# A two-layer attention and convolution kernel: the first attention of layer 1 as a pipeline of two tiles, a new order at the seam of the layers, and the 3x3's weights prepared on VectorE alone

## The chip, the cores and the metric

The kernel runs on one core of a Trainium2 chip. A core has five engines that run their own instruction queues side by side and wait for one another through semaphores: TensorE (PE in the profile; its weight loads are PEld), VectorE (DVE), ScalarE (ACT), GpSimd (POOL) and SyncE (SP), which here only issues DMA transfers. The metric is the time of one execution on the device in microseconds; lower is better. Everything is fp32, apart from some operands of layer 0 that are rounded to fp32r.

## What is computed

The input is x of shape (2, 256, 64, 64): two images ("batches") of 256 channels and 4096 positions. Two layers follow each other, each with a group norm in front and a residual sum behind. Layer 0 is ordinary attention with 8 heads over all 4096 positions. Layer 1 is a mix of two branches (cut to what matters here):

```python
# layer 0: 8 heads, softmax over 4096 keys, residual
q, k, v = split(qkv_w @ groupnorm(x) + qkv_b)
x = x + softmax(q^T k * d**-0.5) v
# layer 1, on y = groupnorm(x)
q, k, v = conv1x1(y), conv1x1(y), conv1x1(y)
# first attention: 64 sets of 64 positions, one from each 8x8 block
ctx   = sa(blockify(q * hd**-0.5 + pos), blockify(k + pos), blockify(v))
feats = relu(conv1x1(ctx) * scale + shift)
# second attention: within each 8x8 block; q and k from two layers of conv1x1+bn+relu
ctx2  = sa(qx(feats), kx(feats), conv1x1(feats))
att   = relu(conv1x1(ctx2) * scale + shift)
# convolution branch: q, k, v mixed by fc, then a grouped 3x3
conv  = grouped_conv3x3(mix(q, k, v, fc_w), dep_w)
out   = x + rate1 * att + rate2 * conv
```

The kernel folds q, k, v, the mixing and the grouped 3x3 into one dense 3x3 convolution whose weights it works out itself from fc, dep and the three 1x1 weights.

## The kernel before, in words

The image is held as 8 tiles of 512 positions (T) with the channels as 2 chunks of 128 partitions (KC). The batches run one after the other, and each goes through the same stages:

1. **Start and projections of layer 0** (`group_stats`, `project0`): statistics on VectorE (L326, L330), means over a group and variances by small matmuls with a constant matrix (pm_l L333, pv_l L343), a square root on ScalarE (L346), normalised tokens xn (L368), then keys, values and queries (p_wk L418 is the first). In batch 0, `fold_scores` (L227 to L242) stands ahead of the statistics; it multiplies small weight matrices together for the first attention of layer 1, which is 1,150 us later.
2. **Attention of layer 0**: 16 groups of a head and half of the queries, 32 blocks of keys each. Scores (L511), exp on ScalarE (L517), values av (L527). The sums of rows for softmax are added up by VectorE (L564) and by accumulating DMAs, then summed over partitions by matmuls with ones (`sum_rows`).
3. **The seam** (`finish_last` from L620, `layer1_first` from L1088): the last group's sums of rows (tile `rows`), their reciprocal (L638), a copy that is kept (L639), the scaled values plus the residual (L641, L642), statistics of these (L644), and the aggregate (L330). Then means and variances again, and x is normalised into `xg` in the order that the first attention wants (L1100 on ScalarE, L368 on VectorE). The first channel chunk can be normalised before the second, whose statistics end last. In batch 0, `fold_products` (pt_w, pm_w, pt_fv, pm_fv, pb_lr, L263 to L283) is mixed in: it multiplies the layer's weight matrices.
4. **First attention of layer 1** ("lr"): 8 tiles. For a tile: py (L1134, L1138, the folded query and key projection of `project`), sp (L1029, L1035, scores), pvs (L1011, values), a softmax on VectorE and ScalarE (nm L1043, e L1045, exp L1046, den L1048 and L1049, e L1050), at (L1055, a transpose of the probabilities), bd (L1064, its copy to a block form by VectorE), pc (L1073, values weighted) and the output `feats` (L1084). The order on TensorE is written out by hand: scores, values and the first half of the next tile's projection, then at, the second half, then pc. `group_attention` is a generator, and each `next` emits one of its parts.
5. **The weights of the 3x3** (`conv_weights`, batch 0 only): it has no hand-written place; the scheduler puts its instructions beside the lr stage, after the last normalisation. For each half m of the output channels and each of 9 taps it adds 12 terms of 128x256 numbers. Six taps are on VectorE (first term L868, then L870), three on GpSimd (L864, L866). The inputs wx of the second half come by DMA (L857) into the place of the first. Further sums (L874 to L881) turn the taps into a form with fewer multiplications, which goes to DRAM (`wf_kept`).
6. **Second attention of layer 1** ("sr", `layer1_second` from L1219): 8 tiles, each with phq, prq, phk, prk (L1267, L1275: two layers for queries and keys), sp, pvs, softmax, at, bd and pc as above. Between a tile's parts stand up to three turns of the convolution (`conv_step`: 32 matmuls mm L948, sums on VectorE L954 to L973; the inputs are transformed by GpSimd, L934 and L938). There are 16 turns, four for two tiles, and the tuple `steps` says how many go with each tile. A tile's output (L1318, DMA L1321) goes out once its attention and the four turns of its pair are done. `fetch_conv_weights` loads the weights from DRAM and, in batch 0, transforms them once more (pw L907, L912).

The next batch's x is loaded tile by tile (L70) into a pool with 9 buffers of a tile each. So tile 0 of batch 1 has a buffer of its own, and tile t takes the one that tile t−1 of batch 0 leaves when its output has been summed. The issues of these loads and of the outputs share one queue, SyncE's, in program order.

On TensorE, and in the seam on ScalarE and VectorE too, the order is that of the code (`manual_schedule`); elsewhere the scheduler of the compiler decides. All functions that the change touches:

## Time and profile before

| what | before |
|---|---|
| median of 3 runs | 3199.27 us (3195.14 to 3202.82) |
| span of the profiled run, granted TensorE clock | 3198.2 us, 0.984 |
| first p_wk of batch 0 | 29.63 us |
| last exp of batch 0's layer 0, first py | 1158.25, 1184.35 us |
| batch 0: first attention of layer 1, from py to the end of the last pc | 1184.35 to 1342.95 us |
| batch 0: second attention, from phq to the end of the last pc | 1345.06 to 1644.45 us |
| batch 1: first p_wk | 1649.81 us |
| batch 1: first attention of layer 1 | 2794.33 to 2907.5 us |

A row of a timeline reads: start, length in us, engine, line, operation, output and inputs with their shapes, how many of the same kind in a row, and in brackets the idle time of the engine before it and what ended that. A row of groups by line reads: line, engine, operation, shapes, count, then busy time in us and the mean of one in ns, then idle time before, with what ended it. The window table gives each engine's busy time in a stretch and the granted clock as a share of full speed. In the page's second section each digit is a fortieth of the span (80 us) in tenths.

The matmul times add up to 96% of the span. Layer 0 takes 71% of the span (29.63 to 1160 us and 1649.81 to 2779 us) and is alike in both batches. What differs between the batches are the first attention of layer 1 (158.6 us against 113.2 us) and the start (the first projection comes 29.63 us after the program's start, and 5.36 us after the end of batch 0).

### The profile page before, as it was taken

How to read it: one execution, taken by the hardware profiler on the slowest of the kernel's cores; microseconds unless marked ns; L12 is line 12 of the kernel's file. 1: busy time of each engine (PE TensorE's matmuls, PEld its weight loads, DVE VectorE, ACT ScalarE, POOL GpSimd, SP SyncE). 2: the span in 40 equal slices, each digit the busy share in tenths (PEclk: the TensorE clock that was granted, in tenths of full speed). 3: DMA queues.
4: the chain of work that ended last, by engine and by line, in shares of the span. 5: the costliest groups of instructions: out<-in, count | busy, mean ns of one | idle time of the engine just before them, and what ended most of it. 6: DMA issues, size and time to landing. Idle time of an engine off the chain costs nothing. (4 is left out here: it accounts for less than half of the span.)

```text
span 3198.2 us, 62765 instructions
## 1 busy us (share of the span) xinstructions
PE 3077.4 (96%) x25107; PEld 1844.3 (58%) x25107; DVE 2492.2 (78%) x3133; ACT 2311.5 (72%) x2365; POOL 927.3 (29%) x1061
## 2 busy tenths in 40 slices
PE   7999999999999988899999999999999999899998
PEld 4455555555555545576755555555555555466766
DVE  4599999999999988747554889989999999824543
ACT  2699999999999972432234899999999999834222
POOL 2122222222222226734300222222222222204530
PEclk9999999999999998899999999999999999999999
DMA  6968779678795651211039686787967875600000
GB/s 241 269 131 174 150 159 183 135 168 176 159 191 129 137 116 48 86 53 53 27 130 275 139 177 142 169 162 155 186 143 164 182 159 119 172 1 8 20 14 22
DMA packets 242710, 425.75 MB, mean 133 GB/s; under 512 B 99164, under 2 KB 109984, under 8 KB 239976
## 3 DMA queue, kind: packets, MB, share of 16 engines
q0 software_dynamic: 96240, 240.41, 37.7%
q1 hardware_dynamic: 146168, 181.24, 20.2%
q8 instruction: 199, 3.26, 0.4%
q14 instruction: 103, 0.84, 0.1%
HBM read 118.52 MB, written 68.12 MB: 58 GB/s over the span
## 5 line engine op out<-in xcount | busy, mean ns | idle before, releaser
L564 DVE TENSOR_TENSOR e<-e,es 128x1024 f32<-128x1024 f32 (+1 forms) x952 | 1035.9, 1144 | 90.2 <-ACT es L517 88.9
L527 PE MATMUL av<-es,v 128*32 128x256 f32 (+1 forms) x9644 | 746.5, 390 | 0.0
L564 DVE TENSOR_TENSOR e<-e,v 128x1024 f32<-128x1024 f32 (+1 forms) x640 | 676.7, 1110 | 50.9 <-ACT v L517 49.0
L517 ACT ACTIVATE es<-sa 128x1536 f32<-128x1536 f32 (+1 forms) x444 | 635.7, 1432 | 96.5 <-PE sa L511 53.4
L511 PE MATMUL sa<-q,k 128*128 128x512 f32 x1736 | 561.1, 430 | 15.0 <-ACT es L517 5.4
L527 PE MATMUL av<-v 128*32 128x256 f32 (+1 forms) x6228 | 507.4, 390 | 0.0
L527 PEld LDWEIGHTS av<-es,v 128*32 128x32 f32 x9644 | 316.2, 109 | 299.4 <-issue 160.8
L511 PEld LDWEIGHTS sa<-q,k 128*128 128x128 f32 x1736 | 280.0, 188 | 298.5 <-issue 142.6
L511 PE MATMUL sc<-q,k 128*128 128x512 f32 x1180 | 371.8, 396 | 4.6 <-ACT es L517 3.5
L511 PE MATMUL sb<-q,k 128*128 128x512 f32 x1180 | 370.8, 395 | 0.3 <-ACT es L517 0.3
L527 PEld LDWEIGHTS av<-v 128*32 128x32 f32 x6228 | 216.8, 109 | 179.2 <-issue 81.7
L517 ACT ACTIVATE es<-sc 128x1024 f32<-128x1024 f32 x296 | 306.8, 1036 | 2.7 <-PE sb L511 2.7
L517 ACT ACTIVATE v<-sc 128x1024 f32<-128x1024 f32 x294 | 304.9, 1037 | 0.0
L517 ACT ACTIVATE es<-sb 128x1024 f32<-128x1024 f32 x296 | 301.9, 1020 | 1.8 <-DMA acc<-es 1.8
L517 ACT ACTIVATE v<-sb 128x1024 f32<-128x1024 f32 x294 | 299.9, 1020 | 0.0
L511 PEld LDWEIGHTS sc<-q,k 128*128 128x128 f32 x1180 | 210.4, 188 | 75.3 <-ACT es L517 14.7
L511 PEld LDWEIGHTS sb<-q,k 128*128 128x128 f32 x1180 | 221.0, 188 | 54.8 <-ACT es L517 2.5
L574 POOL DMA_DIRECT2D es<-es x118 | 101.2, 858 | 496.7 <-ACT es L517 432.5
L517 ACT ACTIVATE v<-sa 128x1536 f32<-128x1536 f32 (+1 forms) x146 | 209.2, 1433 | 35.0 <-PE sa L511 15.1
L948 PE MATMUL mm<-v,wf 128*128 128x256 f32 x1024 | 229.4, 383 | 4.0 <-DVE z L957 4.0
L938 POOL TENSOR_TENSOR v<-col 128x512 f32<-128x512 f32 x128 | 162.1, 1293 | 217.3 <-PE sp_sr L1029 49.5
L948 PEld LDWEIGHTS mm<-v,wf 128*128 128x128 f32 x1024 | 194.6, 191 | 39.0 <-issue 12.9
(260 smaller groups left out, 3357.1 us busy)
## 6 DMA issues: line engine op xcount, KB each, us to landing
acc<-es POOLq DMA_DIRECT2D x130, 512.0 KB, 6.1
acc<-v POOLq DMA_DIRECT2D x84, 512.0 KB, 6.0
es<-es POOLq DMA_DIRECT2D x138, 256.0 KB, 4.0
v<-es POOLq DMA_DIRECT2D x134, 256.0 KB, 4.8
k<-wk_halves SPq DMA_DIRECT2D x64, 512.0 KB
q<-wq_halves SPq DMA_DIRECT2D x256, 128.0 KB
v<-v POOLq DMA_DIRECT2D x90, 256.0 KB, 5.1
es<-v POOLq DMA_DIRECT2D x86, 256.0 KB, 3.8
```

Source lines behind the costliest of these rows:

```text
L511: nc.tensor.matmul(sc[:, i, :], held["k", g // 2][:, j * P : (j + 1) * P], held["q", g, u // 2][:, u % 2, :], start=True, stop=True,)
L517: nc.scalar.activation(dst, sc[:, i : i + m, :], AF.Exp, scale=SC0)
L527: nc.tensor.matmul(dst[HD0 * u : HD0 * u + HD0, n], lhs, rhs(u)[:, n], start=start, stop=stop)
L564: nc.vector.tensor_add(dst[:, s, :], dst[:, s, :], src)
L574: nc.gpsimd.dma_start(out=dst, in_=src, accum_op=ALU.add)
L938: (nc.gpsimd.tensor_add if plus else nc.gpsimd.tensor_sub)(dst, rows(one), rows(two))
L948: nc.tensor.matmul(mm[:, m, r, :], wf[:, k, 4 * r + q, m * P : (m + 1) * P], v[r // 2][:, r % 2, k, :], start=k == 0, stop=k == KC - 1,)
```

## The change

Six edits:

1. `fold_scores` goes behind the projections of layer 0, still in batch 0.
2. In the last group of layer 0 the sums of rows are taken ahead of the values of the last two blocks of keys. ScalarE keeps its copy first, and VectorE takes the reciprocal from that copy in SBUF; the copy of the values follows.
3. The order at the seam: three tiles of the first chunk are normalised on GpSimd, the means and variances of the second chunk stand after two steps of the fold instead of after four, the fold's other steps between them and behind them, and two tiles of the second chunk on ScalarE in both batches.
4. The first attention of layer 1 runs as a pipeline of two tiles: at and pc of tile t−1 come after the scores and values of tile t and beside the projections of tile t+2. The projections of tiles 0 and 1 come first.
5. All nine taps of the weights of the 3x3 are on VectorE, in order.
6. In batch 0 no turn of the convolution goes with tile 1; the weights are fetched in tile 2, and the 16 turns are distributed as (0, 0, 2, 3, 3, 3, 3, 2) instead of (0, 3, 3, 3, 3, 2, 2, 0).

```diff
--- before.py
+++ after.py
@@ -576,7 +576,8 @@
         def work_of(g, j):
 
 
-            add_rows(g, j)
+            if (g, j) < (last, NJ - 2):
+                add_rows(g, j)
             for part in (None,) if j in (0, NJ - 1) else range(2):
                 if part == 1:
                     yield
@@ -627,17 +628,16 @@
             p = g % 2
 
             nc.scalar.activation(st.rstd[:, first_chunk], st.d[:, first_chunk], AF.Sqrt, bias=eps)
-            rows = psum["sc"].tile([P, 3, T], F32, tag="sa", name=f"rows_{b}")[:, 0, :]
-            sum_rows(g, rows)
-            avs = copied[g]
+            rows, avs = held["rows"], copied[g]
             nc.vector.reciprocal(st.rstd[:, first_chunk], st.rstd[:, first_chunk])
             shift = small.tile([P, KC], F32, tag="gn_shift", name=f"shift_{b}")
             st.shift = shift
             shift_of(st, 0)
             kept = w4([P, T], f"kept_{b}")
-            nc.vector.reciprocal(avs[:, 1, :], rows)
             nc.scalar.copy(kept, rows)
+            nc.vector.reciprocal(avs[:, 1, :], kept)
             y = avs[:, 0, :]
+            nc.scalar.copy(y, sums[g])
             nc.vector.tensor_mul(y, y, avs[:, 1, :])
             nc.vector.scalar_tensor_tensor(y, y, bv_last, held["x_last"], ALU.add, ALU.add)
             some = small.tile([P, 6], F32, tag="gn_some", name=f"some_{b}")
@@ -735,6 +735,12 @@
 
             for done in range(NH0 * 2 * NJ):
                 g, j = divmod(done, NJ)
+                if (g, j) == (last, NJ - 2):
+                    assert len(places) == n_units
+                    held["rows"] = psum["sc"].tile([P, 2, T], F32, tag="sb", name=f"rows_{b}")[:, 1, :]
+                    for i in (NJ - 2, NJ - 1):
+                        add_rows(g, i)
+                    sum_rows(g, held["rows"])
                 for _ in work_of(g, j):
                     yield done
                 if g and j == 0:
@@ -755,7 +761,8 @@
                 if j == NJ - 1:
                     waiting.append(g)
                     avs = w4([P, 2, T], f"avs_{b}_{g}")
-                    nc.scalar.copy(avs[:, 0, :], sums[g])
+                    if g < last:
+                        nc.scalar.copy(avs[:, 0, :], sums[g])
                     copied[g] = avs
                     late[:] = [finish(g)]
                     next(late[0])
@@ -855,16 +862,11 @@
         for m in range(2):
             for q in range(3):
                 nc.gpsimd.dma_start(out=wx[:, 4 * q : 4 * q + 4, :], in_=a["wx"][q, m].rearrange("i p c -> p i c"))
-
-            for tap in (6, 0, 1, 7, 2, 3, 8, 4, 5):
-                acc, term = taps[:, tap, :], new_rows[:, 0, :]
+            for tap in range(9):
+                acc = taps[:, tap, :]
                 for i in range(12):
                     src, s = wx[:, i, :], weff[:, m, i, tap : tap + 1]
-                    if tap >= 6:
-                        nc.gpsimd.tensor_mul(acc if i == 0 else term, src, s.to_broadcast([P, C]))
-                        if i:
-                            nc.gpsimd.tensor_add(acc, acc, term)
-                    elif i == 0:
+                    if i == 0:
                         nc.vector.tensor_scalar(acc, src, s, None, ALU.mult)
                     else:
                         nc.vector.scalar_tensor_tensor(acc, src, s, acc, ALU.mult, ALU.add)
@@ -1093,14 +1095,14 @@
 
         xg = apool.tile([P, KC, 64, 8, 8], F32, tag="A", name=f"xg_{b}")
 
-        def to_groups(k, t, act):
+        def to_groups(k, t, eng):
             dst = xg[:, k, :, t, :].rearrange("p (d e) o -> p d e o", d=8)
             src = xts[t][:, k, :].rearrange("p (d o e) -> p d e o", d=8, o=8)
-            if act:
+            if eng is nc.scalar:
                 return nc.scalar.activation(
                     dst, src, AF.Identity, bias=shift[:, k : k + 1], scale=rstd[:, k : k + 1]
                 )
-            return normalise(dst, src, k, mean, rstd)
+            return eng.tensor_scalar(dst, src, mean[:, k : k + 1], rstd[:, k : k + 1], ALU.subtract, ALU.mult)
 
 
         feats = [
@@ -1162,59 +1164,71 @@
             st.aggregate(second)
             fold = fold_products() if b == 0 else iter(())
             put(nc.gpsimd.tensor_copy, (0, 1))
-
-
-            ahead = (1, 1, 1, 1, 0) if b == 0 else (0,) * 7
-            for t, n in enumerate(ahead):
-                to_groups(0, t, True)
-                for _ in range(n):
-                    next(fold)
-                if t == (3 if b == 0 else 4):
-                    put(nc.scalar.copy, (2, 3))
+            for t in range(5, NT):
+                to_groups(0, t, nc.gpsimd)
             pm, pv = bank([P, 1], f"pm_l1_{b}"), bank([P, 1], f"pv_l1_{b}")
+            to_groups(0, 0, nc.scalar)
+            next(fold, None)
+            to_groups(0, 1, nc.scalar)
+            next(fold, None)
             st.means(second, pm, nc.vector.tensor_copy)
             st.spread(second)
+            to_groups(0, 2, nc.scalar)
+            if b == 1:
+                to_groups(0, 3, nc.scalar)
+            next(fold, None)
             st.variances(second, pv)
             st.deviations(second, pv)
             shift_of(st, 1)
-            for t in range(len(ahead), NT):
-                to_groups(0, t, True)
-            n_act = 1 if b == 0 else 2
+            for _ in range(2):
+                next(fold, None)
+            for t in range(3 + b, 5):
+                to_groups(0, t, nc.scalar)
+            put(nc.scalar.copy, (2, 3))
+            n_act = 2
             for t in range(NT):
-                done = to_groups(1, t, t < n_act)
+                done = to_groups(1, t, nc.scalar if t < n_act else nc.vector)
             for _ in fold:
                 pass
             check()
             for i in range(2):
                 open_pair(i)
-            for m in range(KC):
-                project(0, m, slice(0, 1))
-            for m in range(KC):
-                project(0, m, slice(1, KC))
+            for t in range(2):
+                for m in range(KC):
+                    project(t, m, slice(0, 1))
+            for t in range(2):
+                for m in range(KC):
+                    project(t, m, slice(1, KC))
             at_grid(0)
         with tc.manual_schedule(engines={E.PE}):
-            for t in range(NT):
-                def to_feats(m, pc, t=t):
-                    bn_relu(
-                        feats[m][:, :, t, :].rearrange("p o e -> p e o"), pc.rearrange("p (e o) -> p e o", e=8),
-                        V_LR, m,
+
+            before = None
+            for t in range(NT + 1):
+                parts = None
+                if t < NT:
+                    def to_feats(m, pc, t=t):
+                        bn_relu(
+                            feats[m][:, :, t, :].rearrange("p o e -> p e o"),
+                            pc.rearrange("p (e o) -> p e o", e=8), V_LR, m,
+                        )
+
+                    rows = slice(HD0 * (t % 4), HD0 * (t % 4) + HD0)
+                    parts = group_attention(
+                        f"lr_{b}_{t}", tiles.pop(t), source(t),
+                        lambda c, w, t=t: source(t)[:, c, w * P : (w + 1) * P], wts["w3"], to_feats, b == 0,
+                        more=(ats[rows, t // 4, :], grid[rows, :], t == 0),
                     )
-
-                rows = slice(HD0 * (t % 4), HD0 * (t % 4) + HD0)
-                parts = group_attention(
-                    f"lr_{b}_{t}", tiles.pop(t), source(t),
-                    lambda c, w, t=t: source(t)[:, c, w * P : (w + 1) * P], wts["w3"], to_feats, b == 0,
-                    more=(ats[rows, t // 4, :], grid[rows, :], t == 0),
-                )
-                if t in (1, 2):
-                    open_pair(t + 1)
-                if t == 3:
-                    at_grid(1)
+                    next(parts)
+                    if t in (0, 1):
+                        open_pair(t + 2)
+                    if t == 3:
+                        at_grid(1)
                 for m in range(KC):
-                    next(parts)
-                    if t + 1 < NT:
-                        project(t + 1, m, slice(0, KC))
-                next(parts, None)
+                    if t + 2 < NT:
+                        project(t + 2, m, slice(0, KC))
+                    if before:
+                        next(before, None)
+                before = parts
 
         load_set(b, ("fq1", "fk1", "fv"))
         if b == 0:
@@ -1244,7 +1258,7 @@
         ahead = {0: conv_transform(b, xp, *turns[0])}
         done = 0
 
-        steps = (0, 3, 3, 3, 3, 2, 2, 0) if b == 0 else (3, 3, 2, 2, 2, 2, 2, 0)
+        steps = (0, 0, 2, 3, 3, 3, 3, 2) if b == 0 else (3, 3, 2, 2, 2, 2, 2, 0)
 
         def conv():
             nonlocal done
@@ -1284,7 +1298,7 @@
                 for tt in {0: (3, 4)}.get(t, (t + 4,)):
                     if tt < NT:
                         to_image(tt)
-                if t == steps.index(max(steps)):
+                if t == sum(n == 0 for n in steps[:-1]):
                     wf = fetch_conv_weights(b)
                 if steps[t] > 0:
                     conv()
@@ -1327,14 +1341,14 @@
         xts = x_first if b == 0 else load_x(b)
         w0 = w0_first if b == 0 else load_layer0(b)
         with tc.tile_pool(name=f"ps0_{b}", bufs=8, space=PSUM) as psum["ps"]:
-            if b == 0:
-                fold_scores()
             mean, rstd = group_stats(xts, f"l0_{b}")
             xn = apool.tile([P, KC, N], F32, tag="A", name=f"xn_{b}")
             for t in range(NT):
                 for k in range(KC):
                     normalise(xn[:, k, t * T : (t + 1) * T], xts[t][:, k, :], k, mean, rstd)
             held = project0(b, xn, w0)
+            if b == 0:
+                fold_scores()
         if b == 0:
             load_layer1()
             later.extend([lambda t=t: stack_positions(t) for t in range(NT)])
```

## The prediction, made before the changed kernel had run

> **What bounds the kernel now.** I read the page first (shares and the 40 slices), then TensorE's timeline for each stage that the change touches, then the other engines' timelines where TensorE waits, and last the groups by line. The page, sections 1 and 2:
>
> ```profile
> PE 3077.4 (96%) x25107; PEld 1844.3 (58%) x25107; DVE 2492.2 (78%) x3133; ACT 2311.5 (72%) x2365; POOL 927.3 (29%) x1061
> ...
> PE   7999999999999988899999999999999999899998
> DVE  4599999999999988747554889989999999824543
> PEclk9999999999999998899999999999999999999999
> ```
>
> TensorE sets the time: it is below 9 tenths in the first slice, in slices 15 to 17 (batch 0's seam and first attention of layer 1), in 35 (batch 1's seam) and in the last. Only there can this change gain much. The windows table compares that attention in batch 0 and batch 1, then the second attention of batch 0:
>
> ```profile
> 1184.00:1343.00 159.00, 130.62 (x784) 84.37 (x784) 147.91 (x288) 45.38 (x64) 103.48 (x147) 0.83 0.13 39
> 2794.00:2908.00 114.00, 111.79 (x784) 72.32 (x784) 32.33 (x75) 42.48 (x58) 0.78 (x6) 0.97 0.03 8
> 1345.00:1645.00 300.00, 290.37 (x1360) 203.49 (x1360) 154.92 (x322) 95.45 (x139) 120.75 (x85) 0.98 0.16 58
> ```
>
> Columns after the window's length: PE, PEld, DVE, ACT, POOL busy, then granted clock. The same 784 matmuls take 114 us in batch 1 and 159 in batch 0, where VectorE is busy 148 of 159 us and the clock is 0.83. TensorE's timeline of batch 0 says who makes it wait (start, length, what, and in brackets the idle time before and what ended it):
>
> ```profile
> 1209.71 0.66 PE L1055 MATMUL at_lr<-ident,e_lr 128*128 128x128 f32 x2 [6.99 <-DVE e_lr L1050]
> 1247.68 0.66 PE L1055 MATMUL at_lr<-ident,e_lr 128*128 128x128 f32 x2 [3.50 <-DVE e_lr L1050]
> 1288.46 3.75 PE L1073 MATMUL pc_lr<-bd,vs_lr 128*128 128x128 f32 x16 [3.08 <-DVE bd L1064]
> 1296.28 6.28 PE L1011 MATMUL pvs_lr<-wt_w,xg 128*128 128x256 f32 x16
> ```
>
> The waits of the stage add to 28 us, each on a softmax operation queued among the preparation of the 3x3's weights. After a wait matmuls are slow: pvs 6.28 us, 3.72 elsewhere; pc 3.75 against 2.05. The preparation, from the groups by line:
>
> ```profile
> L870 DVE SCALAR_TENSOR_TENSOR prep<-prep 128x256 f32<-128x256 f32 x132 | 97.5, 783 | 0.2
> L866 POOL TENSOR_TENSOR prep<-prep 128x256 f32<-128x256 f32 x66 | 52.1, 789 | 5.0
> L864 POOL TENSOR_TENSOR prep<-prep 128x256 f32<-128x256 f32 x72 | 48.4, 675 | 30.9 <-DVE prep L845 23.2 <-DMA prep<-in_wx_dram 2.9
> ```
>
> From 1251 to 1256 us, where GpSimd is idle, the same L870 starts every 0.40 us instead of 0.80.
>
> **What the Trainium skill says.** "SBUF — State Buffer", Who interferes with whom: a VectorE instruction with two SBUF inputs contends with a GpSimd instruction that reads SBUF, and the later one blocks. The trace agrees (0.80 against 0.40 us). "TensorE: Matmul & The Clock Gate", What's actually happening: the array runs at half clock after some 3.4 us of idleness and needs about as long a busy time to come back; the 6.28 and 3.72 us agree roughly (1.7 times). "ScalarE: Activation LUTs", What ACT_TABLE_LOAD costs: 1283 ns; here 1.28 us. "DMA: Bandwidth & Descriptors", Anatomy of one DMA: a DMA's wait for a semaphore is held in the issuing sequencer; so a load queued behind a write that is not ready waits with it, which the boundary below depends on.
>
> **Part 1, the start** (fold_scores behind project0).
>
> ```profile
> 20.62 0.34 PE L227 MATMUL pt_place<-ident,place_rows 4*128 4x4 f32 x2 [20.62 <-DMA place_rows<-in_posq_dram]
> 26.61 0.36 PE L333 MATMUL pm_l<-mv_l,group 128*128 128x2 f32 x2
> 27.24 1.28 ACT L346 ACT_TABLE_LOAD   x1
> ```
>
> VectorE has its statistics at 15.87; pm_l now goes at 15.95, not 26.61. The table load, hidden today, then waits for pv as at 1647.35 in batch 1, so the first p_wk is at about 20.3 instead of 29.63: 9.3 us. The fold's 6.0 us of matmuls come back after the last projection, 2.93 us of them in an idle time there; some 2 go to copies and the table load before the first exp. 9.3 − 6.0 + 2.9 − 2.2 = **4 us gained** (3 to 6).
>
> **Part 2, the seam of batch 0** (sums of rows ahead of values, order).
>
> ```profile
> 1164.65 3.36 DVE L638 RECIPROCAL avs<-rows 128x512 f32<-128x512 f32 x1 [1.75 <-PE rows L527]
> 1177.79 0.16 DVE L334 COPY mean_l<-pm_l 128x1 f32<-128x1 f32 x1 [5.96 <-PE pm_l L333]
> ```
>
> The sums' matmuls now wait for the last row additions, with the values of the last two blocks queued behind them; those values end only y's sum, so nothing that ends late waits for them. The rows end near 1162.7 instead of 1164.56; the copy goes first (0.6), then the reciprocal (3.36) and the chain of 5 us: aggregate near 1171.5. pm_l then need not queue behind the fold (pt_fv, pm_fv): about 1171.8 instead of 1177.41. Normalising chunk 1 (seven of 0.67 on VectorE, 1.3 on ScalarE) then ends near 1179, against py at 1184.35: 5.4 us. Chunk 0's tiles 5 to 7 on GpSimd are done beside.
>
> **Part 3, the pipeline of batch 0.** Batch 1's timeline from the end of its first pa (2804.57) to its last pc (2907.5) is 102.9 us, 1.42 of it waiting. Tile 1's projections (4.7) are now ahead: 96.8 us of matmuls are left from the end of pa, which is near 1193.0. at and pc of a tile come a whole tile (12.86 us) after its scores. VectorE per tile: 23 to 24 preparation operations at 0.40 (9.4) and softmax (2.7), 12.1 in all: it just fits, as no GpSimd operation runs beside. Were it to run at the 0.48 us that each shows instead of its spacing, it would not: rival (a). I take 0.40, since spacing is what a queue feels. I add 7 us of waits: about 2 where the second half of the inputs arrives (VectorE idles 7.1 us there today), 2.8 at the end where nothing is left to fill, the rest for the low clock. Last pc near 1296.8, against 1342.95. Parts 2 and 3: **46 us gained** (38 to 50).
>
> **Part 4, what is pushed into the second attention.** 216 operations at 0.40 are 86 us where VectorE did 144 with GpSimd's 72 taps beside. 60 of them stand, by instruction order, behind tile 7's bd and ahead of the second attention's first softmax: 24 us, plus 5 as GpSimd's transforms (L934 2.14, L938 1.24 each) run beside for 11 us; then 12 us of the rest and that softmax ahead of bd. Tile 0 takes 38 us, not the 20.7 of an undisturbed tile: +17.3. Tile 1 has no convolution to fill its softmax wait (2.63 in tile 0 today) and starts cold: +4.8. Then 16 turns of 6.91, pw 7.0 and six tiles fit in as now, with 5.4 of waits. Undisturbed, the stage is 8 × 20.7 + 110.6 + 7.0 = 283.2. So 283.2 + 17.3 + 4.8 + 5.4 = 310.7 against 299.4: **11 us lost** (4 to 16). The weights land near 1350 and are needed near 1369: no wait.
>
> **Part 5, the boundary of the batches.** Steps end in 2, not 0: the last convolution stands in tile 7.
>
> ```profile
> 1624.07 0.38 SPq L1321 DMA_DIRECT2D out_dram<-res_sr  x1
> 1624.50 0.47 SPq L70 DMA_DIRECT2D x<-in_x_dram  x1
> 1629.05 1.29 DVE L326 BATCH_NORM_STATS2 stats_l<-x 128x6 f32<-128x512 f32 x2 [3.92 <-DMA x<-in_x_dram]
> 1649.81 2.93 PE L418 MATMUL p_wk<-xn,wqk 128*128 128x512 f32 x3 [2.54 <-DVE xn L368]
> ```
>
> Batch 1's last tile of x takes a buffer that tile 6's output frees. Today that is 20 us before TensorE ends (1644.45), and the gap to p_wk is 5.4 us. Now the last convolution's sums, borders and both outputs come after it on VectorE (8 us), and the load stands behind both writes on the queue: issued 10.5 us after that convolution, landed at 15 (4.5 as above), pm_l at 17; table load and normalisation, 4.5 as at 1645.3 to 1649.8: 21.5. TensorE still has 4.1 us (at, pc) after it, so the gap is 17.4: **12 us lost** (8 to 15).
>
> **Batch 1** has the new seam and pipeline without preparation: py 0.8 earlier and 1.2 at the end: **2 us gained** (0 to 4).
>
> The sum: 4 + 46 − 11 − 12 + 2 = 29; 3199.3 − 29 = **3170 us**.
>
> **Rivals.**
> (a) VectorE becomes the bound of the pipeline. If an operation costs its shown 0.48 us instead of the spacing 0.40, a tile needs 24 × 0.48 + 2.7 = 14.2 us, 1.4 over 12.86, for seven tiles 10, and some 4 more at a low clock: 3184. For it: 148 busy of 159 now. Against: the spacing from 1251 to 1256.
> (b) The losses are hidden: the load goes out early enough and the prepared weights do not delay softmax. Without 12 and half of the 11: 3152. Against: instruction order puts both there.
> (c) Slower than before. VectorE's operations stay at 0.8 us in the second attention and the pipeline stalls: half of part 3's gain goes (+20), tile 0 takes 24 longer and the weights come after 1369, which stalls the first convolution by 10 (+34 − 5 already counted), boundary as above: 3170 + 49 = 3219. Against: GpSimd has work for only 11 us there.
>
> **How the numbers follow.** Main case 0.58, (a) 0.20, (b) 0.14, (c) 0.08. Faster by over 0.2% (below 3192.9): all of the first three but a little of (a)'s upper end: 0.89; within 0.2% 0.04; slower 0.07. The range reaches to (b)'s and past (a)'s value: 3151 to 3188.
>
> **What would show it.** p_wk near 20; pm_l near 13 us after the last exp; no wait over 2 us before at of tiles 0 to 4; 12.9 us per tile; the second attention's tile 0 near 38 us with TensorE waiting for VectorE; a wait of statistics on the x load at the boundary, near 17 us of TensorE idle. Wrong it would be if preparation runs at 0.8 us, or if TensorE waits for convolution weights in tile 2.

## The result: 29.5 us faster, as forecast, with one step of the sum on the wrong side

The changed kernel takes 3168.9 us (median of 4 runs, 3168.4 to 3170.4), the kernel before 3198.4 us: a ratio of 0.9908, with a 95% interval of 0.9891 to 0.9925. Forecast were 3170 us.

The page of the changed kernel, sections 1 and 2 (busy times; then tenths of 40 slices):

```profile
PE 3056.7 (97%) x25107; PEld 1832.7 (58%) x25107; DVE 2467.7 (78%) x3204; ACT 2304.5 (73%) x2359; POOL 856.5 (27%) x929
...
PE   7999999999999999799979999999999999899998
DVE  4599999999999988745645999889999999824543
PEclk9999999999999999899989999999999999999999
```

TensorE's dip has gone from slices 15 and 16. Slice 17, at 8 tenths before, is at 7 (the second attention's first tile), and slice 21 has a new dip (the boundary of the batches). The stages, each from its mark in the timelines of before and of after (us):

| stage | before | after | change | forecast |
|---|---|---|---|---|
| start to the load of exp's table | 118.1 | 113.6 | −4.5 | −4 |
| batch 0, to the end of the last exp | 1040.2 | 1038.8 | −1.4 | 0 |
| batch 0, seam, to the first py | 26.1 | 20.4 | −5.7 | −5.4 |
| batch 0, first attention, to the end of pc | 158.6 | 115.3 | −43.3 | −41 |
| batch 0, on to the end of the second attention | 301.5 | 312.4 | +10.9 | +11 |
| boundary, to p_wk | 5.4 | 15.7 | +10.3 | +12 |
| batch 1, to the end of the last exp | 1127.2 | 1126.7 | −0.6 | 0 |
| batch 1, seam | 17.3 | 17.1 | −0.1 | −0.8 |
| batch 1, first attention | 113.2 | 116.0 | +2.8 | −1.2 |
| batch 1, rest | 290.7 | 290.7 | 0 | 0 |

The changes add to −31.4 us, the difference of the two profiled spans. Five stages carry it: the start, batch 0's seam and its two attentions, and the boundary. First, the windows of the changed kernel that answer to those of before (columns: PE, PEld, DVE, ACT, POOL busy, granted clock, DMA share, GB/s):

```profile
1172.00:1289.00 117.00, 112.11 (x784) 72.54 (x784) 100.63 (x284) 49.73 (x69) 3.04 (x9) 0.98 0.16 49
2760.00:2877.00 117.00, 112.07 (x784) 72.53 (x784) 31.91 (x75) 45.02 (x61) 2.19 (x7) 0.98 0.02 7
1290.00:1601.00 311.00, 290.04 (x1360) 203.80 (x1360) 174.65 (x385) 95.13 (x138) 137.17 (x85) 0.97 0.16 59
```

In the first attention of batch 0 TensorE is busy for 112 of 117 us at a clock of 0.98, the same as in batch 1, although VectorE still has 101 us of work beside. The 3x3's preparation, from the groups by line of the changed kernel, and TensorE's timeline in that stage:

```profile
L872 DVE SCALAR_TENSOR_TENSOR prep<-prep 128x256 f32<-128x256 f32 x198 | 88.7, 503 | 0.2
```

```profile
1248.33 0.44 PE L1057 MATMUL at_lr<-ident,e_lr 128*128 128x128 f32 x2
1268.25 3.72 PE L1013 MATMUL pvs_lr<-wt_w,xg 128*128 128x256 f32 x16
1273.23 2.02 PE L1075 MATMUL pc_lr<-bd,vs_lr 128*128 128x128 f32 x16 [1.04 <-DVE bd L1066]
```

198 operations take 88.7 us where 132 took 97.5. The waits of up to 7 us ahead of at and pc are gone; three of 1.0 to 1.2 us are left at the end of the stage. The start and the seam (timelines of PE and DVE):

```profile
17.05 0.59 PE L333 MATMUL pm_l<-mv_l,group 128*128 128x2 f32 x2 [17.05 <-DVE mv_l L330]
21.54 16.97 PE L418 MATMUL p_wk<-xn,wqk 128*128 128x512 f32 x32 [2.48 <-DVE xn L368]
```

```profile
1157.66 3.35 DVE L638 RECIPROCAL avs<-kept 128x512 f32<-128x512 f32 x1 [2.79 <-ACT kept L637]
1165.79 0.16 DVE L334 COPY mean_l<-pm_l 128x1 f32<-128x1 f32 x1 [0.48 <-PE pm_l L333]
```

What was lost is in the second attention's tile 0 (timeline of PE):

```profile
1320.63 0.69 PE L1057 MATMUL at_sr<-ident,e_sr 128*128 128x128 f32 x2 [11.65 <-DVE e_sr L1052]
1327.67 3.43 PE L1075 MATMUL pc_sr<-bd,vs_sr 128*128 128x128 f32 x16 [2.94 <-DVE bd L1066]
```

and at the boundary (timeline of SyncE's queue, then of VectorE and TensorE):

```profile
1604.13 1.67 SPq L1335 DMA_DIRECT2D out_dram<-res_sr  x2
1605.84 0.52 SPq L70 DMA_DIRECT2D x<-in_x_dram  x1
```

```profile
1609.82 1.29 DVE L326 BATCH_NORM_STATS2 stats_l<-x 128x6 f32<-128x512 f32 x2 [4.43 <-DMA x<-in_x_dram]
1611.75 0.56 PE L333 MATMUL pm_l<-mv_l,group 128*128 128x2 f32 x2 [11.17 <-DVE mv_l L330]
```

TensorE waits 11.65 us for the softmax that stands behind the preparation, and 11.17 us for the statistics of a tile of x whose load went out 5.3 us after the last matmul of the batch (1600.58). Before, it went out 20 us ahead of it.

### The profile page after: what moved, and what is told of

It is laid out like the page before. It is cut to its first block, busy times and chain, and to the rows that moved or that the text cites. A ratio compares the mean times of both kernels' runs of the same rounds, so it can differ in the third digit from the quotient of the medians.

```text
span 3166.8 us, 62680 instructions
## 1 busy us (share of the span) xinstructions
PE 3056.7 (97%) x25107; PEld 1832.7 (58%) x25107; DVE 2467.7 (78%) x3204; ACT 2304.5 (73%) x2359; POOL 856.5 (27%) x929
## 3 DMA queue, kind: packets, MB, share of 16 engines
q1 hardware_dynamic: 146168, 181.24, 20.3%
```

## The experiments

Each run has a total that compares with 3168.9 us, and stages from its profile. The stages are the better witness: in these profiles layer 0 of batch 0 alone varies between 1038.4 and 1043.8 us, though no edit but those of its last group touches it. The totals were taken in several sets, and the kernel before, run again in each, had medians from 3196.8 to 3200.1 us; so a difference of 3 us between two totals shows nothing by itself. All runs (us; layer 0 from the load of exp's table, in batch 1 from p_wk, to the end of the last exp):

| run | layer 0, both batches | seam, batch 0 | first attention, batch 0 | to the end of the second | boundary | first attention, batch 1 | total, median |
|---|---|---|---|---|---|---|---|
| before | 1040.2, 1127.2 | 26.1 | 158.6 | 301.5 | 5.4 | 113.2 | 3198.4 |
| after | 1038.8, 1126.7 | 20.4 | 115.3 | 312.4 | 15.7 | 116.0 | 3168.9 |
| pipeline undone | 1040.0, 1126.3 | 21.0 | 118.4 | 313.7 | 15.9 | 113.6 | 3171.2 |
| taps on GpSimd again | 1039.2, 1126.6 | 21.0 | 155.2 | 298.3 | 16.1 | 116.0 | 3193.6 |
| last turn earlier | 1039.2, 1126.4 | 21.4 | 115.7 | 316.7 | 5.4 | 115.9 | 3162.2 |
| old turns | 1038.4, 1125.9 | 21.0 | 114.5 | 328.9 | 5.4 | 116.3 | 3173.7 |
| fold_scores first | 1042.0, 1127.5 | 21.4 | 115.9 | 312.5 | 16.1 | 115.7 | 3179.7 |
| rows as before | 1041.9, 1128.0 | 21.8 | 114.3 | 313.7 | 16.0 | 115.5 | 3172.2 |
| seam's order as before | 1038.8, 1127.9 | 21.1 | 115.0 | 310.9 | 16.0 | 115.5 | 3168.7 |
| both as before | 1038.7, 1127.6 | 25.6 | 116.0 | 311.0 | 16.2 | 116.1 | 3173.4 |
| end of the pipeline reordered | 1043.3, 1127.4 | 21.4 | 113.4 | 317.6 | 15.9 | 113.0 | 3171.2 |
| GpSimd held back | 1043.8, 1129.8 | 19.4 | 114.3 | 320.7 | 16.2 | 116.4 | 3184.2 |
| GpSimd behind bd | 1043.8, 1130.4 | 21.6 | 115.2 | 304.9 | 16.9 | 115.5 | 3171.0 |
| combined | 1040.7, 1128.7 | 21.6 | 115.2 | 308.5 | 5.4 | 112.2 | 3155.3 |

Two of these kernels, "end of the pipeline reordered" and "combined", weight one tile with another tile's probabilities, as the section on the end of the pipeline shows. Their times are those of such programs.

### Which part brings the 43 us: the pipeline or the taps on VectorE alone

The pipeline alone undone:

```diff
-            for t in range(2):
-                for m in range(KC):
-                    project(t, m, slice(0, 1))
+            for m in range(KC):
+                project(0, m, slice(0, 1))
...
-                    if t + 2 < NT:
-                        project(t + 2, m, slice(0, KC))
-                    if before:
-                        next(before, None)
-                before = parts
+                    next(parts)
+                    if t + 1 < NT:
+                        project(t + 1, m, slice(0, KC))
+                next(parts, None)
```

> The changed kernel (3168.9 us) with the pipeline of two tiles alone undone: at and pc of a tile follow its own scores again, and only tile 0 is projected ahead; the taps stay on VectorE alone. My theory: the contention with GpSimd was the main cause of the waits; with operations at 0.40 us the softmax chain (2.8 us and some five operations of preparation between its steps, 4.8 us) almost fits behind pvs and half a projection (6.0 us), and about 1 to 1.5 us per tile is left. First attention of layer 1 in batch 0 8 to 14 us longer than 115 us, total 3175 to 3183. Rival: the order on TensorE is what removes the waits; 25 to 35 us longer, total 3193 to 3203.

Measured: 3171.2 us, under my own theory's range and far from the rival's. The stage is 118.4 us, 3.1 longer, where 8 to 14 were expected. Two of its waits, from TensorE's timeline:

```profile
1192.27 0.44 PE L1057 MATMUL at_lr<-ident,e_lr 128*128 128x128 f32 x2 [0.68 <-DVE e_lr L1052]
1265.13 3.40 PE L1075 MATMUL pc_lr<-bd,vs_lr 128*128 128x128 f32 x16 [1.49 <-DVE bd L1066]
```

With operations of 0.40 us the softmax chain fits nearly everywhere behind pvs and half a projection. Now the opposite, the pipeline kept and three taps back on GpSimd:

```diff
-            for tap in range(9):
+            for tap in (6, 0, 1, 7, 2, 3, 8, 4, 5):
...
+                    if tap >= 6:
+                        nc.gpsimd.tensor_mul(acc if i == 0 else term, src, s.to_broadcast([P, C]))
+                        if i:
+                            nc.gpsimd.tensor_add(acc, acc, term)
```

> The changed kernel with three of the nine taps on GpSimd again, all else kept, the pipeline too. My theory: VectorE runs at 0.8 us an operation while GpSimd works (about 100 us), the order puts some 23 operations into each tile, so VectorE bounds the stage: 20 to 35 us longer than 115 us; the second attention's tile 0 gets back to about 27 us (11 less); total 3178 to 3195. Rival: the slack of a whole tile hides the slow operations; the stage is under 6 us longer, tile 0 is 11 shorter, total 3159 to 3165, faster than the changed kernel.

Measured: 3193.6 us, inside my theory's range; the stage is 155.2 us, 40 longer, where 20 to 35 were expected, and what follows is 14 shorter. Its window, the operation's group and two waits on TensorE:

```profile
1172.00:1328.00 156.00, 126.82 (x784) 84.92 (x784) 145.98 (x277) 48.28 (x69) 103.25 (x147) 0.84 0.14 40
```

```profile
L876 DVE SCALAR_TENSOR_TENSOR prep<-prep 128x256 f32<-128x256 f32 x132 | 96.2, 777 | 0.2
```

```profile
1217.94 3.76 PE L1079 MATMUL pc_lr<-bd,vs_lr 128*128 128x128 f32 x16 [9.75 <-DVE bd L1070]
1291.30 3.75 PE L1079 MATMUL pc_lr<-bd,vs_lr 128*128 128x128 f32 x16 [5.33 <-DVE bd L1070]
```

VectorE is busy for 146 of 156 us, the operation takes 777 ns again, and a whole tile of slack does not hide it: the queue in front of bd is longer than a tile. Of the 40 us some 15 are the same 784 matmuls taking longer (126.8 us busy against 112.1, at a granted clock of 0.84 against 0.98); the rest is waiting. So the two runs settle it: 40 of the 43 us come from taking GpSimd away from beside VectorE, and the pipeline brings 3, with GpSimd (158.6 to 155.2 us, the kernel before against this run) as without it (118.4 to 115.3). Most of that it gives back in batch 1 (116.0 against 113.6 us without it).

### What the new turns cost and save

```diff
-        steps = (0, 0, 2, 3, 3, 3, 3, 2) if b == 0 ...
+        steps = (0, 0, 3, 3, 3, 3, 3, 1) if b == 0 ...
```

> The changed kernel with the turns of batch 0 as (0, 0, 3, 3, 3, 3, 3, 1): the last turn of tile 7 stands ahead of its keys' branch, not ahead of at and pc. My theory: the load of the last tile of x goes out some 14 us earlier, the gap between the batches falls from 15.7 to 5.4 us, total 3158 to 3160. Rival: the gap is not due to the last turn but to the two output writes ahead of the load on the queue; the gap stays over 12 us, total within 3 us of 3168.9.

Measured: 3162.2 us, above my theory's 3158 to 3160. The boundary is 5.4 us, as in the kernel before, so the last turn is what delayed the load. From SyncE's queue: the load now goes out 11 us ahead of TensorE's end (1605.77).

```profile
1594.19 0.39 SPq L1335 DMA_DIRECT2D out_dram<-res_sr  x1
1594.64 0.46 SPq L70 DMA_DIRECT2D x<-in_x_dram  x1
```

Only 6.7 of the 10.3 us are left in the total. The second attention became 4.2 us longer: without a turn between the scores and at, tile 7 waits 2.5 us for bd instead of 1.7 and runs cold (pc 3.56 against 2.02 us), and earlier tiles have two small waits too (1.5 us for bd at 1438.54 and 0.5 us for a turn at 1496.55). Then the old turns in the changed kernel:

```diff
+        steps = (0, 3, 3, 3, 3, 2, 2, 0) if b == 0 ...
```

> The changed kernel with the old distribution of turns (0, 3, 3, 3, 3, 2, 2, 0) and so the weights used in tile 1. The weights are in place near 1343 us in the changed kernel (load issued at 1331.6, some 11 us), and pw would stand at about 1338. My theory: a wait of 5 to 8 us for the weights in tile 1, but tile 1 has turns to fill its softmax wait (2.6) and the gap between the batches falls back to 5.4 (10.3): total 3161 to 3166, so the new distribution loses more at the boundary than it saves. Rival: the turns of tile 1 wait longer for weights or buffers, 10 us or more, and the new distribution is needed: total 3169 or above.

Measured: 3173.7 us. The boundary is 5.4 us, but the second attention lost 16.4. The wait for the weights is as expected,

```profile
1346.61 9.92 PE L909 MATMUL pw<-ident,wf 128*128 128x128 f32 x64 [5.47 <-DMA wf<-wf_kept]
1485.55 8.72 PE L950 MATMUL mm<-v,wf 128*128 128x256 f32 x32 [3.95 <-DVE z L959]
```

and I had missed two others: the 3.95 us stall of a turn on VectorE, which the kernel before has at 1515.19 too and the changed kernel does not, and five more in tile 0, where GpSimd now prepares a second turn beside VectorE's last operations. So the rival was nearer: the new distribution is worth its loss at the boundary, and moving its last turn forward is better than either.

### The start

```diff
+            if b == 0:
+                fold_scores()
             mean, rstd = group_stats(xts, f"l0_{b}")
...
             held = project0(b, xn, w0)
-            if b == 0:
-                fold_scores()
```

> The changed kernel with fold_scores ahead of the statistics again. My theory: the start is worth the 5.9 us by which the last exp of batch 0's layer 0 moved (1158.25 to 1152.37), so p_wk is near 29.6 again and the total 3173 to 3176. Rival: part of the 5.9 us came from elsewhere in layer 0, and the total rises by 4.0 us or less, the predicted value, to at most 3172.9.

Measured: 3179.7 us, 10.8 more than the changed kernel; both expectations were too low. In its profile exp's table is loaded 6.6 us later (120.12), at 118.08 in the kernel before, and layer 0 takes 3.2 and 0.8 us more. The first 4.5 us of that are what the edit had brought. Another 2.2 us are in TensorE's timeline: with the fold first, TensorE's first matmul waits for a transfer, and in this profile that landed at 22.82 us, in the kernel before at 20.62.

```profile
22.82 0.34 PE L227 MATMUL pt_place<-ident,place_rows 4*128 4x4 f32 x2 [22.82 <-DMA place_rows<-in_posq_dram]
```

The 4 us in layer 0 have no cause that these traces show; they stay open.

### The seam: two edits that do the same

First the rows alone undone, then the order alone (both cut):

```diff
-            if (g, j) < (last, NJ - 2):
-                add_rows(g, j)
+            add_rows(g, j)
...
-            nc.scalar.copy(kept, rows)
-            nc.vector.reciprocal(avs[:, 1, :], kept)
+            nc.vector.reciprocal(avs[:, 1, :], rows)
+            nc.scalar.copy(kept, rows)
```

> The changed kernel with the sums of rows of the last group behind the values again, and the reciprocal ahead of the copy. My theory: the rows end 1.7 us earlier in the changed kernel (4.6 instead of 6.3 us after the last exp), but the reciprocal now waits for the copy (0.6), so the aggregate comes only 0.6 us earlier in each batch; undone, 1 to 2 us are lost in both batches together, total 3170 to 3171. Rival: the whole 1.7 us counts in both batches, total 3172 to 3173.

```diff
-            st.means(second, pm, nc.vector.tensor_copy)
...
+            ahead = (1, 1, 1, 1, 0) if b == 0 else (0,) * 7
+            for t, n in enumerate(ahead):
+                to_groups(0, t, True)
+                for _ in range(n):
+                    next(fold)
...
+            st.means(second, pm, nc.vector.tensor_copy)
```

> The changed kernel with the old order at the seam (means of the second chunk behind four steps of the fold, no tile on GpSimd, one tile of the second chunk on ScalarE in batch 0). My theory: pm_l queues behind the fold again, some 5 us after the aggregate instead of 0.1, so batch 0 loses 4 to 6 us and batch 1 nothing, total 3173 to 3175. Rival: the normalisation sets the first py in both orders; under 2 us lost, total up to 3171.

Measured: 3172.2 us without the rows' edit, with a seam of 21.8 us (and of 17.5 in batch 1, against 17.1); 3168.7 us without the order's, with 21.1. Of nine other runs that keep both edits, eight have 21.0 to 21.6, one has 19.4. So the order by itself brings nothing, against my theory, and the rows by themselves about half a microsecond in each batch; the first total lies where the rival had it, but its layer 0 is 3.1 and 1.3 us longer, and the seam is not. Yet together they took 4 to 5 us away. A new theory, tested with both undone:

> The changed kernel with both edits of the seam undone: sums of rows behind the values, reciprocal ahead of the copy, and the old order of means, fold and normalisation. Each alone cost at most 1.4 us of the 5.7 us by which the seam of batch 0 became shorter (20.4 to 21.8 us from the last exp to the first py, against 26.1). New theory: they do the same thing twice; the copy ahead of the reciprocal lets the fold start 8.5 us earlier, and the new order takes the means out from behind the fold, so either is enough. Then both undone give 25 to 26.5 us in batch 0's seam, total 3173 to 3176. Rival: the 5.7 us come from something else (the earlier end of the layer, the projections of two tiles); the seam stays under 23 us, total up to 3172.

Measured: 3173.4 us and a seam of 25.6 us, as the new theory had it. TensorE's timelines, first of the kernel with the order alone undone, then with both undone:

```profile
1160.17 0.66 PE L263 MATMUL pt_w<-ident,wt_w 128*128 128x128 f32 x4 [1.11 <-ACT avs L640]
1166.87 0.28 PE L333 MATMUL pm_l<-mv_l,group 128*128 128x1 f32 x2
```

```profile
1162.15 0.66 PE L263 MATMUL pt_w<-ident,wt_w 128*128 128x128 f32 x4 [4.12 <-ACT kept L639]
1170.39 0.28 PE L333 MATMUL pm_l<-mv_l,group 128*128 128x1 f32 x2
```

The last exp ends at 1152.75 and 1151.72. With the copy first, ScalarE reads the rows without waiting for the reciprocal, the fold starts 7.4 us after the last exp instead of 10.4, and pm_l follows at 14.1 instead of 18.7, even behind the fold. With the new order only two of the fold's steps stand ahead of pm_l: in the run with the rows alone undone the fold also starts 10.4 us after the last exp (1164.37 against 1153.94), and pm_l comes at 14.8. Either is enough.

### The end of the pipeline

```diff
             for t in range(NT + 1):
                 parts = None
+                drain = NT - 2 <= t < NT
+                if drain:
+                    next(before)
...
+                if t == NT - 1:
+                    next(parts)
                 for m in range(KC):
```

> The changed kernel with the end of the pipeline reordered on TensorE: where no projection is left to stand between at and pc (tiles 5, 6 and 7), at of the tile before goes ahead of the scores, and at of tile 7 ahead of pc of tile 6. My theory: the three waits for bd (1.42, 1.44 and 1.06 us in batch 1) go, batch 1's first attention of layer 1 falls from 116.0 to 112.3 us; in batch 0 (1.04, 1.04, 1.15) it shortens too, but tile 0 of the second attention waits for VectorE's preparation anyway, so nothing of it counts: total 3164 to 3166. Rival: both batches gain, 6 to 7 us, total 3162 to 3163; or the waits come back elsewhere, within 1 us of 3168.9.

The waits that it is after, in batch 1 of the changed kernel:

```profile
2860.86 2.02 PE L1075 MATMUL pc_lr<-bd,vs_lr 128*128 128x128 f32 x16 [1.42 <-DVE bd L1066]
2870.76 2.02 PE L1075 MATMUL pc_lr<-bd,vs_lr 128*128 128x128 f32 x16 [1.44 <-DVE bd L1066]
2874.06 2.02 PE L1075 MATMUL pc_lr<-bd,vs_lr 128*128 128x128 f32 x16 [1.06 <-DVE bd L1066]
```

Measured: 3171.2 us, outside both expectations, but the stages speak clearly. Batch 1's first attention falls to 113.0 us, 2.9 less, with one wait of 1.42 left:

```profile
2870.20 0.86 DVE L1066 COPY bd<-at_lr 64x256 f32<-64x256 f32 x2 [1.31 <-PE at_lr L1057]
2877.03 0.85 DVE L1066 COPY bd<-at_lr 64x256 f32<-64x256 f32 x2
2878.02 3.81 PE L1075 MATMUL pc_lr<-bd,vs_lr 128*128 128x128 f32 x32 [1.42 <-DVE bd L1066]
```

These lines show a fault of this order that I had overlooked. The kernel has one buffer for bd (`bds = [bd, bd]`). Tile 6's probabilities are written into it at 2870.20 and tile 7's at 2877.03, and only then come the 32 matmuls of pc for both tiles: tile 6 is weighted with tile 7's probabilities. In a right order bd of tile 7 would have to wait for pc of tile 6, or have a buffer of its own; no run has that, so how much of the 2.9 us remains then is not shown. In batch 0 it is 2 us shorter, and the second attention 5.2 longer: there VectorE's queue sets when tile 0 ends. From the first py to pc of tile 0 are 154.9 us in the changed kernel and 157.2 here; what TensorE saves ahead of it, it waits there (20.10 us for the softmax instead of 11.65), since the softmax's last step now stands behind the preparation's last operation on VectorE. The layer 0 of this profile is 4.5 us longer.

### The preparation's tail in the second attention

GpSimd held back until the preparation has ended, by a copy that reads its last result:

```diff
+        gate = const.tile([P, 1], F32, name="gate")
+        kept["gate"] = nc.gpsimd.tensor_copy(gate, new_cols[:, 3, 1, 0:1])
...
-        ahead = {0: conv_transform(b, xp, *turns[0])}
+        with tc.issue_after(kept["gate"].ins):
+            ahead = {0: conv_transform(b, xp, *turns[0])}
```

> The changed kernel with GpSimd's first transform of the convolution in batch 0 held back until the preparation of the weights has ended (a copy of one column by GpSimd is added for that). In the changed kernel GpSimd's first L936 lies open for 20 us beside VectorE's preparation and then VectorE's operations take 1.4 to 2.4 us each for about 10 us. My theory: those 10 us are contention; without GpSimd every operation takes 0.40, at of tile 0 comes about as now, but bd right behind it: 5 to 6 us gained, total 3162 to 3165. Rival: VectorE's work ahead of bd sets the time whatever GpSimd does, or the transforms then come too late for the first turn: within 1.5 us of 3168.9 or slower.

First the changed kernel's timelines of GpSimd and VectorE in tile 0:

```profile
1289.46 20.07 POOL L936 TENSOR_TENSOR col<-xp 128x1152 f32<-128x1152 f32 x1 [7.05 <-ACT xp L1249]
```

```profile
1298.15 7.20 DVE L872 SCALAR_TENSOR_TENSOR prep<-prep 128x256 f32<-128x256 f32 x18
1307.45 2.36 DVE L872 SCALAR_TENSOR_TENSOR prep<-prep 128x256 f32<-128x256 f32 x1
1309.73 1.47 DVE L882 TENSOR_TENSOR prep<-prep 128x256 f32<-128x256 f32 x1
```

then VectorE's of the run:

```profile
1309.08 0.48 DVE L872 SCALAR_TENSOR_TENSOR prep<-prep 128x256 f32<-128x256 f32 x1
1322.32 7.96 DVE L986 TENSOR_SCALAR x<-x,edges 128x8 f32<-128x8 f32 x13
```

Measured: 3184.2 us, worse; of the 16.4 us between the two profiles, 8.3 are in the second attention and 8.0 in layer 0 of the two batches. The contention was real: the preparation ends 30.2 us after the first attention instead of 38.6. But the scheduler then put some two dozen small additions at the image's borders ahead of the softmax, and GpSimd, now free, works beside those: 0.61 us each, where twelve of them take 1.71 us in all in the changed kernel. So both expectations missed a third thing. It was taken out (cut):

```diff
-        ahead = {0: conv_transform(b, xp, *turns[0])}
+        ahead = {} if b == 0 else {0: conv_transform(b, xp, *turns[0])}
...
+            if b == 0 and t == 0:
+                gate = const.tile([P, 1], F32, name="gate")
+                held_back = nc.gpsimd.tensor_copy(gate, bds[(turn[0] - 1) % 2][:, 0, 0, 0:1])
+                with tc.issue_after(held_back.ins):
+                    ahead[0] = conv_transform(b, xp, *turns[0])
+            with tc.issue_after(kept["bd"].ins):
-            conv_edges(xts, t)
+                conv_edges(xts, t)
```

> The changed kernel with GpSimd's first transform in batch 0 held back until bd of the second attention's tile 0 (by a copy of one column of bd on GpSimd), and with the additions at the image's borders behind bd on VectorE. In the kernel that held GpSimd back until the preparation had ended, the preparation ended 30.2 us after the first attention instead of 38.5, but the border additions then stood ahead of the softmax and took 0.6 us each beside GpSimd. My theory: with both out of the way pc of tile 0 starts 31 to 33 us after the end of the first attention instead of 39.5, and 6 to 8 us are gained, total 3161 to 3163. Rival: what is saved there comes back, since the transforms of the first turns then come late or tile 1 has the contention instead: total within 2 us of 3168.9 or above.

```profile
1325.31 2.92 PE L1075 MATMUL pc_sr<-bd,vs_sr 128*128 128x128 f32 x16 [2.92 <-DVE bd L1066]
```

Measured: pc of tile 0 starts 32.0 us after the first attention (1293.29) instead of 39.5, and the whole second attention is 7.6 us shorter: the theory, in its stage. The total, 3171.0 us, is where the rival had it, but not for the rival's reason: layer 0 is 5.0 and 3.7 us longer than in the changed kernel (4.9 and 3.1 in the run before), and in both runs the accumulating transfers of layer 0 land later. The last column is the median time to landing in us, for the changed kernel and then for this run:

```profile
acc<-es POOLq DMA_DIRECT2D x130, 512.0 KB, 6.1
acc<-v POOLq DMA_DIRECT2D x84, 512.0 KB, 6.0
```

```profile
acc<-es POOLq DMA_DIRECT2D x130, 512.0 KB, 6.4
acc<-v POOLq DMA_DIRECT2D x84, 512.0 KB, 6.4
```

What the two runs share and no other has is a constant of 4 bytes per partition. The last run keeps the gate without it.

### The parts that gain, together

The turns (0, 0, 3, 3, 3, 3, 3, 1), GpSimd and the borders behind bd, and the reordered end in batch 1 alone (cut):

```diff
+                drain = b == 1 and NT - 2 <= t < NT
...
+        steps = (0, 0, 3, 3, 3, 3, 3, 1) if b == 0 ...
...
+                gate = small.tile([P, 4], F32, tag="nm4", name="gate")
```

> The changed kernel with three edits together: the turns of batch 0 as (0, 0, 3, 3, 3, 3, 3, 1); GpSimd's first transform and the border additions behind bd of the second attention's tile 0; and, in batch 1 alone, at of a tile ahead of the scores where no projection is left. The gate that holds GpSimd back is now a tile of an existing pool with the shape of its neighbours, no longer a new constant of 4 bytes per partition. The two runs with that constant had slower accumulating transfers in layer 0 (6.4 us to landing, not 6.0 to 6.2) and a longer layer 0 (1043.8 and about 1130 us from first exp to last, not 1038.6 and 1126.7). My theory: the parts add up (6.7, 7.6 and 2.9 us), and the constant had moved the layout of the buffers, so layer 0 is back at 1038 to 1040 us with landings of 6.0 to 6.2: total 3150 to 3155. Rival: the slow transfers come from GpSimd's or VectorE's new order itself or the gains overlap (the later first transform delays the turns of tile 2); total above 3157.

Measured: 3155.3 us (3153.4 to 3155.7), a ratio to the kernel before of 0.9856 (0.984 to 0.9873): shorter than both kernels, and just above my theory's 3150 to 3155. The landings are 6.1 and 6.0 us again. Against the changed kernel the second attention lost 3.9 us less, the boundary 10.3 and batch 1's first attention 3.8; layer 0 is 1.8 and 2.1 us longer still. The 3.8 us can't be kept as they stand: in batch 1 this kernel too writes tile 7's bd (2857.53) ahead of tile 6's pc (2858.53). Without the reordered end I estimate 3155.3 + 3.8, some 3159 us, from the stages; no run has it.

## Why the prediction was right, point by point

**The bound was read rightly.** TensorE sets the time, and the time went where its slices are below 9 tenths. The windows of before (VectorE 148 of 159 us busy in batch 0, 32 of 114 in batch 1) named the cause, and the run with the taps back on GpSimd shows it.

**Part 1** was forecast at 4 us and is 4.5. p_wk came at 21.5, not 20.3: the last tile of x landed a microsecond later in this profile, and VectorE's aggregate ended with it near 17.0 instead of 15.87. The load of exp's table comes between 111.9 and 114.0 us in the twelve profiles with this edit, so 4.1 to 6.2 us earlier than before.

**Part 2** has the right size (5.4; measured 5.7, and about 4.9 by the other runs' 21.2 us) for half of a reason. The step "pm_l then need not queue behind the fold" is true (of two steps of five it still does), and not needed: the fold itself starts earlier since the copy comes first. The rows ended 1.7 us earlier, against 1.9 forecast. The aggregate, counted from the last exp, came 0.6 us earlier (0.3 forecast): the reciprocal now waits for the copy, and L641 takes 1.23 us beside GpSimd instead of 0.69.

**Part 3** was forecast at 41 us of the 46 and is 43.3: the sum allowed 7 us of waits and 3.2 came, with no trace of the cold clock. The choice of 0.40 us, the spacing, over the shown 0.48 was right (18 operations in 7.20 us), though the stretch from 1251 to 1256 showed it less directly than the text says: there L870 alternates with other operations, and it is the next of these that starts 0.40 us after it. What the text put first, the whole tile between scores and at, is worth 3 us; "no GpSimd operation runs beside" is worth 40.

**Part 4** was forecast at 11 us and is 10.9, by errors that cancel. Tile 0 took 40.4 us (phq to phq, 1290.49 to 1330.90), not 38: "plus 5 as GpSimd's transforms run beside" should have been 8, as the 38.6 and 30.2 us of preparation show. Tile 1 took 23.8 us, not 25.5, and the rest 1.3 us less than the sum allowed. The weights made nobody wait.

**Part 5** was forecast at 12 us and is 10.3. The chain is the one described, link by link: last turn, sums, two outputs, load, statistics, table. The load went out 5.3 us after the last pc instead of 6.4; the run with the last turn earlier shows the cause.

**Batch 1** is where a step failed: "1.2 at the end" was booked as a gain and came out as a loss of 2.8 us. With the projections two tiles ahead, three tiles instead of one have nothing between at and pc, and each waits 1.1 to 1.4 us for bd. The same three waits were counted in batch 0's 2.8 us "at the end where nothing is left to fill", but not carried over to batch 1. The reordered end takes back 2.9, but in an order that is not right.

**The rivals.** (a) did not come: without GpSimd an operation costs its spacing of 0.40 us. What VectorE as the bound looks like is shown by the run with the taps back on GpSimd, at 0.78 us an operation and 3193.6 us. (b) did not come: both losses are in the trace. For (c), VectorE's slow operations in the second attention exist (1.4 to 2.4 us each), but for 10 us, not for 60 operations.

## What to carry to other kernels

Where two engines slow each other down, giving all of the work to one can be faster than sharing it, though that engine is the busier: 216 operations kept VectorE busy for 95 us (88.7 and 6.1), 144 with GpSimd beside for 106. Ask then what stands behind the longer queue, here a softmax of the next stage, and which buffer is freed later because work moved to the end, here a load for the next batch. And look at the last tiles of a pipeline: what filled a wait in the steady state runs out there first. Where an order is changed there, look also at which buffer the next tile overwrites.

## What the runs showed of the hardware that was not expected

**A stream of VectorE operations can keep GpSimd out for 18 us.** In the changed kernel GpSimd's L936, 2.1 to 2.2 us elsewhere, stays open from 1289.46 to 1309.53, while VectorE runs its two-input operations at 0.40 us undisturbed. It ends 2.4 us after the start of VectorE's L881 (1307.12), and from then on each VectorE operation waits for a GpSimd one (1.47 us). Six other runs show the same, with 18.9 to 20.1 us, and in each L936 ends 2.4 us after L881 starts. But it need not come so: in the two runs with the old order at the seam L936 gets in at once, and it is VectorE that is slow right then. In the run with the order alone undone 18 of its operations take 15.06 us there instead of 7.2:

```profile
1289.09 2.49 POOL L936 TENSOR_TENSOR col<-xp 128x1152 f32<-128x1152 f32 x1 [6.10 <-ACT xp L1243]
1286.71 15.06 DVE L872 SCALAR_TENSOR_TENSOR prep<-prep 128x256 f32<-128x256 f32 x18
```

The Trainium skill ("SBUF — State Buffer", Who interferes with whom) says that the one that issues first takes the port for its whole instruction; that a stream of short ones can hold it over many instructions is what the seven traces add. What decides who gets in, and why the hand-over comes at L881, is not settled.

**Small single-input operations suffer too.** The border additions (L986, 128x8) took 0.61 us each beside GpSimd and 0.14 alone. The same section has tensor_scalar among the operations that can take the shared port, where their operands meet its conditions; the traces agree with that.

**Transfers were slower in the two runs with one constant more.** With a constant of 4 bytes per partition more, the accumulating transfers of layer 0 landed in 6.4 us instead of 5.8 to 6.3 in all other profiles, and batch 1's layer 0 took 1129.8 and 1130.4 us, where the others have 1125.9 to 1128.7. With the gate in an existing pool the landings were back at 6.1 and 6.0. Batch 0's layer 0 was as long (1043.3) in a run with ordinary landings, so its length alone proves nothing. That the addresses of the buffers are the reason is argued from three runs; no run varied them by themselves.
